# A block transpose moved behind the next row's sums, and mix weights loaded in parts

## The chip, the cores and the metric

The kernel runs on one core of a Trainium2 chip. The metric is the device time of one execution in microseconds; smaller is better. The engines are TensorE (PE in the profile, its weight loads PEld), VectorE (DVE), ScalarE (ACT), GpSimd (POOL) and SyncE (SP), which issues nearly all DMA transfers. Each engine works through its own list of instructions in order and waits at an instruction until what it needs is there.

## The reference, cut to what matters

The input x is 32 images of 56 x 56 tokens with 128 channels, all in f32. Two residual layers follow each other.

```
x = x + window_attention(group_norm(x))      # 7x7 windows shifted by 3, 4 heads of 32 channels
x = x + fourier_feedforward(group_norm(x))

window_attention(x):   qkv = x @ w_qkv.T per window of 49 tokens; softmax(q k^T * scale + bias + mask) v; @ w_proj.T + b
fourier_feedforward(x):
    along each of the two image axes: dct, keep 32 modes, mix channels per mode (w0 for one axis, w1 for the other), idct
    h = sum of both;  out = relu(h @ W1 + b1) @ W2 + b2          # 128 -> 512 -> 128
group_norm: 32 groups of 4 channels, statistics over the image
```

w0 and w1 have 128 x 128 x 32 numbers each, 2 MB. In the kernel their first use is in the Fourier layer of the first image.

## The kernel before, in words

Attention works on rows: one row is a strip of 7 lines of an image, 8 windows of 49 tokens, and an image has 8 rows. All images follow each other in one list of 256 rows. A loop over cycles starts one row per cycle and does older rows' later steps beside it. In cycle c:

- `attn_qk`, `attn_scores` and `attn_v` do row c on TensorE. ScalarE and VectorE move q and k out of PSUM (VectorE's half of k is L398), and VectorE adds the bias to the scores into `a` (L440).
- `attn_max` takes the maximum on VectorE (L450), and GpSimd subtracts it (L451). `attn_exp` is ScalarE's exponential (L457). `attn_divide` sums on VectorE (L462), takes the reciprocal (L464), and GpSimd multiplies twice (L467), first into `off_blocks`, then into `own_blocks`. Four SyncE transfers (L475, L476) then copy the 32 x 32 blocks that lie in the wrong partitions from `off_blocks` to `own_blocks`.
- `attn_transpose` is VectorE's block transpose of `own_blocks` into `eT` (L481). It waits for these copies. GpSimd may write `own_blocks` for the next row only when the transpose has read it.
- `attn_values` of row c - 3 multiplies `eT` with v on TensorE (L496), and ScalarE and VectorE move the result to `oT` (L528, L526). `attn_project` follows; VectorE adds it to the tokens in `xl` (L543). `attn_sums` of row c - 4 takes sums (L557) and sums of squares (L566) for the second layer's group norm.

In the first 11 cycles, `first_rows`, there is attention alone; in cycle c the exponential and the sums are those of row c - 1 and the transpose that of row c - 2. From cycle 11 on (`CONV_BEGIN`) the main loop also runs the Fourier layer of the image before: its statistics once per image (`fourier_stats`, a TensorE matmul that needs all L566 of the image), the transforms (L641), the mixing with w1 and w0 (L675), the way back (L714), and from the 9th cycle of an image on the feed-forward in two halves, `ff_in` and `ff_out` (L112), whose result VectorE adds to `res` (L783). Here the exponential and the sums in cycle c are those of row c itself, and the transpose that of row c - 1. The norm of the next image (`image_norm`) is spread over its steps; one of them is the small bias factor nb on VectorE (L362), whose matmul TensorE runs between attn_qk and ff_in.

The order on TensorE, ScalarE, VectorE and GpSimd is the order in which the code calls these functions; it is written by hand (`manual_schedule`). SyncE's order is made by the scheduler. Attention matmuls share four PSUM banks (pa) in rotation, the Fourier layer four others (pc), so a matmul waits until the bank that it gets has been emptied. The constants, w1sb and w0sb among them, are loaded in the order of the code on SyncE's queue (`const_load`, L134), behind image 1's load and ahead of the first row's block copies.

Of the kernel before, what the change touches and what calls it, by code (L numbers as in the profile page):

```python
# [10 lines left out]
F32 = mybir.dt.float32  # L11
# [4 lines left out]
P = 128  # L16
S = 56
C = 128
# [9 lines left out]
NM = 32  # L28
# [20 lines left out]
def swin_fourier_kernel(  # L49
# [20 lines left out]
    nc = tc.nc  # L70
    NB = x.shape[0]

    const = ctx.enter_context(tc.tile_pool(name="const", bufs=1))
# [46 lines left out]
    def load_image(b, parts=2):  # L120
        t = big.tile([TC, NCH, C], F32, tag="xl", name="xl", bufs=2)
        for k in range(parts):
            load_part(t, b, k)
        return t
# [7 lines left out]
    def const_load(shape, src, name):  # L132
        t = const.tile(shape, F32, tag=name, name=name)
        (nc.scalar if name in FIRST else nc.sync).dma_start(t, src)  # L134
        return t
# [21 lines left out]
    with nc.allow_non_contiguous_dma(reason="relative position bias, once"):  # L157
# [4 lines left out]
        for ix in range(WS):  # L162
            src = bass.AP(
                rpb_rev.tensor, rpb_rev.offset + WS - 1 - ix, [[span, NH * span], [1, WS]]
            )
# [44 lines left out]
    with nc.allow_non_contiguous_dma(reason="constant, once"):  # L210
        for blk in range(8):
# [4 lines left out]
            src = idct_h.rearrange("p (h r) -> p h r", r=4)[modes, :, 2 * li : 2 * li + 2]  # L216
# [2 lines left out]
    idcth = idcth.rearrange("p h r -> p (h r)")  # L219
    if NB > 1:  # L220
        xls[1] = load_image(1)
    w1sb = const_load([P, NM, C], w1, "w1sb")
    w0sb = const_load([P, NM, C], w0, "w0sb")
    wff1 = const_load([P, FF], W1, "wff1")
    b1sb = const_load([P, NF], b1.rearrange("(f p) -> p f", p=P), "b1sb")
    wff2 = const_load([P, NF, C], W2.rearrange("(f p) o -> p f o", p=P), "wff2")
# [41 lines left out]
    def image_groups(im, i):  # L268

        pt = [conv_bank() if i % 4 else attn_bank() for _ in range(2)]
        pts = [
            p[:, : n * S].rearrange("p (j r s) -> p j r s", r=n, s=WS) for p, n in zip(pt, (8, 6))
        ]
        for c in range(7):
            nc.tensor.transpose(
                pts[c // 4][:, :, 2 * (c % 4) : 2 * (c % 4) + 2],
                im.x[:, WS * i // 2 + c],
                ident_x[:, :, SS:].rearrange("p r (j s) -> p j r s", s=WS),  # L280
            )
        for k in range(2):

            im.xw[i + k] = big.tile([P, RT + JP - WT], F32, tag="xw", name="xw", bufs=10)
            nc.gpsimd.memset(im.xw[i + k][:, RT:], 0.0)
            xw = im.xw[i + k][:, :RT]
            dst = xw.rearrange("p (j r s) -> p j r s", r=WS, s=WS)
            if k:
                nc.scalar.copy(dst[:, :, 0], pts[0][:, :, WS])
                nc.scalar.copy(  # L290
                    dst[:, :, 1:].rearrange("p j r s -> p j (r s)"),
                    pts[1].rearrange("p j r s -> p j (r s)"),
                )
            else:
                nc.scalar.copy(
                    dst.rearrange("p j r s -> p j (r s)"),
                    pts[0][:, :, :WS].rearrange("p j r s -> p j (r s)"),
                )
            nc.vector.bn_stats(im.st[:, i + k], xw)
        if im.b > 1:  # L300
            image_bias(im, i)
# [157 lines left out]
    def attn_divide(r):  # L459
        a3 = a_sb[r % 2].rearrange("p t w j -> p (t w) j")  # L460
        sm = small.tile([P, 2 * NWR], F32, tag="sm", name="sm")
        nc.vector.tensor_reduce(sm, a3, axis=AX.X, op=ALU.add)  # L462
        rs = small.tile([P, 2 * NWR], F32, tag="rs", name="rs")
        nc.vector.reciprocal(rs, sm)  # L464
        for dst in (off_sb, own_sb):
            for k, (j0, n) in enumerate(((0, KB), (KB, WT - KB))):
                nc.gpsimd.tensor_tensor(  # L467
                    dst[:, k, :, :n],
                    a3[:, :, j0 : j0 + n],
                    rs.unsqueeze(2).to_broadcast([P, 2 * NWR, n]),  # L470
                    ALU.mult,
                )
        for p in range(0, P, JP):
            lo, hi = slice(p, p + KB), slice(p + KB, p + JP)
            nc.sync.dma_start(own_sb[lo, 1], off_sb[hi, 0])  # L475
            nc.sync.dma_start(own_sb[hi, 0], off_sb[lo, 1])  # L476

    def attn_transpose(im, i):

        eT = work.tile([P, NH * NP, JP], F32, tag="eT", name="eT")  # L480
        nc.vector.transpose(eT.rearrange("p t (k j) -> p k t j", k=2), own_sb)  # L481
        im.eT[i] = eT
# [334 lines left out]
    def row(r):  # L817
        return (images[r // NWR], r % NWR) if 0 <= r < NB * NWR else (None, 0)
# [12 lines left out]
    def load_back(cycle):  # L831
        for im, c in fourier(cycle):
            for width, g in back_groups(c):
                load_modes(im, width, g)
# [36 lines left out]
    def has_ff(cycle):  # L871
        return any(c in FF_AT for _, c in fourier(cycle))
# [37 lines left out]
        if im:  # L910
            attn_values(im, i, cycle - 3)

    def turn(cycle):
        im, i = row(cycle)
        if im:
            attn_transpose(im, i)

    def next_groups(cycle):
        b, i = divmod(cycle, NWR)
        if b + 1 < NB:  # L920
            for j in ({4: (0, 2), 5: (4, 6)} if b == 0 else {6: (0, 2, 4, 6)}).get(i, ()):
                image_groups(images[b + 1], j)
# [6 lines left out]
    def halves_last(cycle, norm):  # L929
        im, i = row(cycle)  # L930
        if im:
            attn_v(im, i, cycle)
        if has_ff(cycle):
            half_columns(cycle)
        half_columns(cycle, True)
        load_back(cycle + 1)
        next_begin(cycle)
        load_first(cycle)
        next(norm, None)
        if row(cycle)[0]:  # L940
            attn_exp(cycle)
            attn_divide(cycle)
        im, j = row(cycle - 3)
        if im:
            last_out(cycle)
            attn_project(im, j)
# [10 lines left out]
    def first_rows(cycle, norm):  # L957
        im, i = row(cycle)
        if im:
            attn_qk(im, i, True)  # L960
        if cycle:
            attn_exp(cycle - 1)
        im3, i3 = row(cycle - 3)
        if im3:
            attn_values(im3, i3, cycle - 3)
        turn(cycle - 2)
        if cycle:
            attn_divide(cycle - 1)
        if im:
            attn_scores(im, i, cycle)  # L970
            attn_max(cycle)
        if im3:
            attn_project(im3, i3)
        next(norm, None)
        last, j = row(cycle - 4)
        if last:
            for _ in attn_sums(last, j):
                pass
        if im:
            attn_v(im, i, cycle)  # L980

        if cycle < NWR // 2:
            image_bias(im, 2 * cycle)
        elif cycle >= NWR - 2 and cycle < NWR + 2:
            image_bias(images[1], 2 * (cycle - NWR + 2))
        if cycle in (4, 5):
            for half in range(2):
                bias_and_mask(nc.gpsimd, 1, cycle - 4, half)
        next_begin(cycle)
        next_groups(cycle)  # L990
        if cycle == CONV_BEGIN - 1:
            start_stats(im3)
            for _ in attn_sums(im3, i3):
                pass
            turn(cycle - 1)
            attn_exp(cycle)
            attn_divide(cycle)

    ET = mybir.EngineType
    with tc.manual_schedule(engines={ET.PE, ET.Activation, ET.DVE, ET.Pool}):  # L1000
        images[0] = image_begin(0)
        for i in range(0, NWR, 2):
            image_groups(images[0], i)
        norm = image_norm(images[0])
        for _ in range(3):
            next(norm)
        for cycle in range(NB * NWR + CONV_BEGIN + FF_AT[-1] - NWR + 1):
            if cycle < CONV_BEGIN:
                first_rows(cycle, norm)
            else:  # L1010
                halves_first(cycle, norm)
                if not row(cycle - 3)[0]:
                    half_columns(cycle)
                    half_columns(cycle, True)
                    load_first(cycle)
                    last_out(cycle)
                    quarters(cycle)
                    load_back(cycle + 1)
                    continue
                if not has_ff(cycle):  # L1020
                    half_columns(cycle)
                eighths(cycle)
                quarters(cycle)
                if not has_ff(cycle):
                    next(norm, None)
                if row(cycle)[0]:
                    attn_max(cycle)
                turn(cycle - 1)
                next_groups(cycle)
                halves_last(cycle, norm)  # L1030
            b, i = divmod(cycle, NWR)
            if i == (NWR - 2 if b else NWR - 3) and b + 1 < NB:
                norm = image_norm(images[b + 1])
                next(norm, None)
# [62 lines left out]
```

## Time and profile before

Three runs took 3543.2, 3557.74 and 3561.03 us; the median is 3557.74. The profiled execution has a span of 3546.4 us.

| engine | busy us | share of the span | instructions |
|---|---|---|---|
| PE | 3361.2 | 95% | 70144 |
| PEld | 2637.0 | 74% | 70144 |
| DVE | 2494.9 | 70% | 4722 |
| ACT | 1992.9 | 56% | 3788 |
| POOL | 1827.4 | 52% | 2204 |

Busy time is the time in which the engine had an instruction at work; what lies between is waiting, and the profile names the instruction on another engine, or the transfer, that ended each wait. In the slices of the span TensorE stands at 4, 6 and 8 tenths in the first three of forty and at 9 in all others. An image takes some 107 us in the steady part, a row 12 to 16 us.

The block transpose is one instruction per row: 256 of them with a mean of 1240 ns, 317.5 us in all. The sums before it in the new order are 963 ns in the mean, the reciprocal 253 ns.

### The profile page before, as it was taken

The numbers are of one execution on the slowest core, as the hardware profiler recorded it, in microseconds if no ns is written. First come the engines' busy times: TensorE is split into PE (matmuls) and PEld (weight loads), VectorE is DVE, ScalarE is ACT, GpSimd is POOL, SyncE is SP. The second block draws the span as 40 slices with busy tenths as digits, with TensorE's granted clock in tenths as the row PEclk, the third lists the DMA queues.
The fourth block names the chain that finished last, engine by engine and source line by source line (L and its number), as shares of the span: only waits on it lengthen the run. The fifth ranks groups of instructions, "written<-read, shape, count | busy, mean of one in ns | idle before, by whom it ended". The sixth has DMA issues, their size and how long they took to land.

```text
span 3546.4 us, 159605 instructions
## 1 busy us (share of the span) xinstructions
PE 3361.2 (95%) x70144; PEld 2637.0 (74%) x70144; DVE 2494.9 (70%) x4722; ACT 1992.9 (56%) x3788; POOL 1827.4 (52%) x2204
## 2 busy tenths in 40 slices
PE   4689999999999999999999999999999999999999
PEld 3567777777777777778777777777777777777776
DVE  4777777777777777776777776777776777777741
ACT  3455555555655555655555555555655555655553
POOL 4655554455555455554555554555554555554521
PEclk8799999999999999999999999999999999999999
DMA  4344555554555545555544555545555545555443
GB/s 116 86 112 118 138 129 142 132 125 127 136 132 143 134 120 132 137 131 138 136 126 128 134 132 135 138 120 135 132 133 137 136 122 131 137 135 135 119 132 98
DMA packets 736503, 457.35 MB, mean 129 GB/s; under 512 B 56351, under 2 KB 673984, under 8 KB 735552
## 3 DMA queue, kind: packets, MB, share of 16 engines
q1 hardware_dynamic: 735197, 446.82, 49.8%
q8 instruction: 551, 9.03, 1.1%
q14 instruction: 144, 1.18, 0.1%
q10 hardware_dynamic: 611, 0.32, 0.0%
HBM read 218.29 MB, written 161.48 MB: 107 GB/s over the span
## 4 chain that ended last, share of the span: by engine, by line
PE 45%; POOL 17%; DVE 13%; issue 10%; DMA 7%; ACT 4%; SPq 4%; POOLq 0%; DVEq 0%; ACTq 0%
PE pc L112 19%; PE pc L641 6%; PE pa L112 5%; POOL own_blocks L467 5%; POOL off_blocks L467 4%; DMA own_blocks<-off_blocks 4%; DVE sm L462 4%; PE pa L410 3%; POOL xl L308 3%; PE pc L675 3%; PE pa L432 3%; POOL a L451 2%; ACT a L457 2%; PE pa L496 2%; SPq L475 2%
## 5 line engine op out<-in xcount | busy, mean ns | idle before, releaser
L451 POOL TENSOR_TENSOR a<-a,mx 128x784 f32<-128x784 f32 x256 | 384.7, 1503 | 904.5 <-DVE mx L450 884.3
L467 POOL TENSOR_TENSOR off_blocks<-a,rs 128x512 f32<-128x512 f32 (+1 forms) x512 | 430.0, 861 | 644.7 <-DVE rs L464 441.6
L112 PE MATMUL pc<-wff,hid 128*64 128x128 f32 x12544 | 741.1, 273 | 4.5 <-issue 3.2
L112 PE MATMUL pc<-xf,wff 128*64 128x512 f32 (+2 forms) x3584 | 719.8, 539 | 1.0 <-DVE xf L725 1.0
L112 PEld LDWEIGHTS pc<-wff,hid 128*64 128x64 f32 x12544 | 703.5, 137 | 11.1 <-issue 5.1
L759 ACT ACTIVATE hid<-pc,b1sb 128x512 f32<-128x512 f32 (+2 forms) x896 | 515.0, 632 | 69.3 <-PE pc L112 67.5
L112 PEld LDWEIGHTS pc<-xf,wff 128*64 128x64 f32 x3584 | 286.0, 137 | 349.2 <-issue 223.2
L481 DVE STREAM_TRANSPOSE eT<-own_blocks 128x1024 f32<-128x1024 f32 x256 | 317.5, 1240 | 190.5 <-DMA own_blocks<-off_blocks 175.9
L467 POOL TENSOR_TENSOR own_blocks<-a,rs 128x512 f32<-128x512 f32 (+1 forms) x512 | 430.1, 862 | 0.0
L462 DVE TENSOR_REDUCE sm<-a 128x16 f32<-128x784 f32 x256 | 246.6, 963 | 254.2 <-ACT a L457 253.4
L112 PE MATMUL pa<-xw,wn 128*64 128x392 f32 (+1 forms) x2048 | 397.5, 503 | 18.6 <-ACT wn L365 9.2
L381 ACT ACTIVATE q<-pa,bqkv 128x392 f32<-128x392 f32 x256 | 149.8, 585 | 452.6 <-PE pa L112 448.4
L457 ACT ACTIVATE a<-a 128x784 f32<-128x784 f32 x256 | 219.0, 856 | 246.3 <-POOL a L451 238.3
L417 ACT COPY v<-pa 128x512 f32<-128x512 f32 x256 | 150.8, 589 | 342.6 <-PE pa L410 341.6
L526 DVE TENSOR_SCALAR oT<-pa,bqkv 128x147 f32<-128x147 f32 (+2 forms) x768 | 171.0, 279 | 219.5 <-PE pa L496 219.5
L747 POOL TENSOR_TENSOR res<-res,b2sb 128x512 f32<-128x512 f32 (+2 forms) x256 | 264.4, 1038 | 110.9 <-DMA res<-scr 102.7
L496 PEld LDWEIGHTS pa<-eT,v 49*32 49x32 f32 x16384 | 174.6, 106 | 167.5 <-issue 125.6
L410 PE MATMUL pa<-wn,xw 128*64 128x128 f32 x4096 | 287.5, 282 | 6.7 <-DVE oT L526 3.0
L308 POOL TENSOR_TENSOR xl<-xl,bproj 112x512 f32<-112x512 f32 (+1 forms) x256 | 287.4, 1146 | 0.0
L440 DVE TENSOR_TENSOR a<-pa,bm 128x392 f32<-128x392 f32 x512 | 264.6, 559 | 23.4 <-PE pa L432 4.2
L112 PE MATMUL pa<-wproj,oT 128*48 128x128 f32 (+1 forms) x3584 | 251.5, 276 | 10.7 <-ACT oT L528 7.3
L410 PEld LDWEIGHTS pa<-wn,xw 128*64 128x64 f32 x4096 | 224.2, 138 | 44.2 <-issue 8.8
(96 smaller groups left out, 5367.6 us busy)
## 6 DMA issues: line engine op xcount, KB each, us to landing
own_blocks<-off_blocks SPq DMA_DIRECT2D x1024, 64.0 KB
zscr<-z SPq DMA_DIRECT2D x512, 112.0 KB
htok<-scr SPq DMA_DIRECT2D x256, 196.0 KB
zT<-zscr SPq DMA_DIRECT2D x192, 256.0 KB
res<-scr SPq DMA_DIRECT2D x160, 256.0 KB
out_dram<-res SPq DMA_DIRECT2D x160, 256.0 KB
scr<-xl SPq DMA_DIRECT2D x128, 224.0 KB
xl<-in_x_dram SPq DMA_DIRECT2D x32, 784.0 KB
```

The source lines that it names most:

```text
L112: nc.tensor.matmul(dst[ps], lhsT=lhsT[:, ps], rhs=rhs, start=start, stop=stop)
L308: nc.gpsimd.tensor_tensor(piece, piece, bproj.unsqueeze(1).to_broadcast([TC, e - a, C]), ALU.add)
L410: nc.tensor.matmul(pv[hs, j * C : (j + 1) * C], lhsT=im.xw[i][:, w * WT : w * WT + JP], rhs=im.w[:, 2 * C : 3 * C], start=True, stop=True,)
L440: nc.vector.tensor_tensor(a[:, 2 * hp : 2 * hp + 2, :, 0:WT].rearrange("p u w j -> p w u j"), ps[hp][:, :RT].rearrange("p (w u j) -> p w u ...
L451: nc.gpsimd.tensor_tensor(a3, a3, mx.unsqueeze(2).to_broadcast([P, 2 * NWR, WT]), ALU.subtract)
L457: nc.scalar.activation(a2, a2, AF.Exp)
L462: nc.vector.tensor_reduce(sm, a3, axis=AX.X, op=ALU.add)
L467: nc.gpsimd.tensor_tensor(dst[:, k, :, :n], a3[:, :, j0 : j0 + n], rs.unsqueeze(2).to_broadcast([P, 2 * NWR, n]), ALU.mult,)
L481: nc.vector.transpose(eT.rearrange("p t (k j) -> p k t j", k=2), own_sb)
L496: nc.tensor.matmul(po4[u][h * HD : (h + 1) * HD, pr], lhsT=v[ks, pr, h * HD : (h + 1) * HD], rhs=eT[ks, h * NP + pr, :WT], start=True, sto ...
L747: nc.gpsimd.tensor_tensor(res[:m, c0:c1], res[:m, c0:c1], b2sb[:m].unsqueeze(1).to_broadcast([m, c1 - c0, C]), ALU.add,)
L759: nc.scalar.activation(hf[:, :n], ph[:, :n], AF.Relu, bias=b1sb[:, f : f + 1])
```

## The change

Two things are changed. First, the transpose of row r - 1 is now called inside `attn_divide` of row r, behind the sums and the reciprocal, in place of its own call ahead of them (`turn`, which goes away). It is meant to let the sums, and with them GpSimd's products, start without waiting for the copies of the row before, and to do the transpose while GpSimd fills `off_blocks`. The last row, which no sums follow, gets a call of its own. Second, w1 and w0 are no longer loaded whole among the constants, but in eight parts of 8 modes each (0.5 MB), one called in each of the cycles 2 to 9, so that the first row's block copies don't stand behind 4 MB.

```diff
-    w1sb = const_load([P, NM, C], w1, "w1sb")
-    w0sb = const_load([P, NM, C], w0, "w0sb")
+    w1sb = const.tile([P, NM, C], F32, tag="w1sb", name="w1sb")
+    w0sb = const.tile([P, NM, C], F32, tag="w0sb", name="w0sb")
+
+    def mix_weights(k):
+        dst, src = ((w1sb, w1), (w0sb, w0))[k // 4]
+        m = slice(k % 4 * NM // 4, (k % 4 + 1) * NM // 4)
+        nc.sync.dma_start(dst[:, m], src[:, m])
...
@@ attn_divide @@
         nc.vector.reciprocal(rs, sm)
+        im, i = row(r - 1)
+        if im:
+            attn_transpose(im, i)
         for dst in (off_sb, own_sb):
...
-    def turn(cycle):
-        im, i = row(cycle)
-        if im:
-            attn_transpose(im, i)
...
@@ halves_last @@
             attn_exp(cycle)
             attn_divide(cycle)
+        elif row(cycle - 1)[0]:
+            attn_transpose(*row(cycle - 1))
...
@@ first_rows @@
-        turn(cycle - 2)
         if cycle:
             attn_divide(cycle - 1)
...
+        if 1 < cycle < 10:
+            mix_weights(cycle - 2)
         if cycle == CONV_BEGIN - 1:
             start_stats(im3)
             for _ in attn_sums(im3, i3):
                 pass
-            turn(cycle - 1)
             attn_exp(cycle)
             attn_divide(cycle)
...
@@ main loop @@
                 if row(cycle)[0]:
                     attn_max(cycle)
-                turn(cycle - 1)
                 next_groups(cycle)
                 halves_last(cycle, norm)
```

## The prediction

> **What bounds the kernel now.** I read the page first, then the windows by stage, then the waits of TensorE, then the timeline row by row. The windows split the span in four: stalled start, first rows, first image's Fourier rows, steady part. Columns: length, busy time of each engine (instructions), granted clock, DMA share, GB/s.
>
> ```profile
> 37.00:61.00 24.00, 3.11 (x51) 1.65 (x51) 1.60 (x2) 3.07 (x5) 3.77 (x4) 0.66 0.90 277
> 61.00:152.00 91.00, 62.88 (x1320) 44.47 (x1318) 66.08 (x131) 37.30 (x72) 66.03 (x87) 0.79 0.22 56
> 152.00:245.00 93.00, 68.52 (x1444) 52.71 (x1444) 67.03 (x131) 46.71 (x93) 47.91 (x60) 0.87 0.45 112
> 245.00:3400.00 3155.00, 3067.45 (x64856) 2420.82 (x64858) 2308.62 (x4335) 1829.67 (x3479) 1673.99 (x2001) 1.00 0.52 132
> ```
>
> From 245 us on TensorE is idle 87.5 us in 3155, under 3%. There every wait of TensorE goes straight into the end time, and nothing on VectorE or GpSimd can win more than that 87.5. Before 245 us no engine is full; a chain of waits sets the pace. The waits (waiter, releaser, total us, times, longest) say which idle is at stake:
>
> ```profile
> DVE sm L462 <- ACT a L457: 253.4, 191, 4.3
> DVE eT L481 <- DMA own_blocks<-off_blocks: 175.9, 110, 23.8
> PE pa L112 <- DVE part L566: 28.4, 30, 1.4
> PE pa L112 <- DVE nb L362: 22.8, 29, 1.7
> PE pa L496 <- DVE eT L481: 19.9, 1, 19.9
> ```
>
> The transpose L481 waits much for its copies, but TensorE waits for the transpose only once, 19.9 us at the start. Its waits for part L566 and nb L362 come once per image in the steady part. The third view is VectorE's timeline around the second layer's statistics of a middle image, with TensorE's line that waits for it:
>
> ```profile
> 1517.36 0.96 DVE L450 TENSOR_REDUCE mx<-a 128x16 f32<-128x784 f32 x1
> 1518.24 1.24 DVE L481 STREAM_TRANSPOSE eT<-own_blocks 128x1024 f32<-128x1024 f32 x1
> 1520.83 0.97 DVE L462 TENSOR_REDUCE sm<-a 128x16 f32<-128x784 f32 x1 [1.35 <-ACT a L457]
> 1521.83 0.25 DVE L464 RECIPROCAL rs<-sm 128x16 f32<-128x16 f32 x1
> 1522.00 0.36 DVE L783 TENSOR_TENSOR res<-pc,res 128x256 f32<-128x256 f32 x1
> ...
> 1524.58 0.68 DVE L566 TENSOR_REDUCE part<-sq 112x32 f32<-112x512 f32 x1
> ...
> 1525.32 0.43 PE L112 MATMUL pa<-part,gmean 112*64 112x64 f32 x4 [1.03 <-DVE part L566]
> ```
>
> Between max and sums VectorE has to wait for GpSimd's subtraction (1.50) and ScalarE's exponential (0.86): some 2.5 us, in which the transpose of 1.24 lies free of charge. After the sums VectorE runs without a gap into the wait of TensorE.
>
> [...] the sums of row 1 had their input at 39.5 us and ran at 60.57, behind the transpose of row 0, which waited 23.83 for a copy. [...] the copies of row 0 landed at 59.3 us behind 4 MB of mix weights issued at 41.7 and 42.2. [...] eight matmuls L112 pa<-xw,wn take 2.88 us at 139.84 (clock 0.50) and 1.49 at 1519.26. [...] so I count TensorE's waits and not its 95%.
>
> **The change part by part.** No instruction is added but six DMA issues; the orders of TensorE, ScalarE and GpSimd stay the same. SyncE's order shifts in places, mostly own_blocks copies going ahead of a store of xl.
>
> *Weights in parts.* Ahead of row 0's own_blocks copies 4.19 MB leave the queue. What stays is image 1's load (1.61 MB), wff1, wff2 (0.52) and b2 (0.06): 2.19 MB at the 277 GB/s of the first window is 7.9 us from 37.2, so 45.1. Then four issues of 0.6 and a landing of 2.0: 49.5, and the transpose ends near 50.7 instead of 60.6. Gain 10 us (8 to 13). The parts are 0.52 MB each, 1.9 us at 277 GB/s. SyncE's order has three of them behind row 0's copies, three behind row 1's and two behind row 2's; those rows lie 7 us or more apart, so 5.7 us of loading fits between them (cost 0 to 2).
>
> *Transpose behind the sums, first rows.* Before, a row is this loop (chain of waits at 65 to 75 us): own_blocks done, SyncE 1.6, copy 2.0, transpose 1.25, sums and reciprocal 1.12, off_blocks 1.67, own_blocks 1.64, with latencies 9.6. Afterwards sums no longer wait for the copy, and the transpose lies beside off_blocks (1.25 beside 1.67). What waits behind the transpose is the score evictions L440, and through their banks the next qk matmuls. The new loop is max, subtract 1.50, exponential 0.86, sums 0.97, reciprocal 0.25, transpose 1.17, two evictions 1.0, max 0.97: 6.7, with latencies 7.0. GpSimd's loop through off_blocks and own_blocks is the same 7. The sums of row 1 are also done while row 0's copy is still out, so own_blocks of row 1 ends at about 53 (before 65.2) and of row 2 at 60 (74.9). From there to row 10, before: 76.9 us for eight rows. Afterwards: rows 3, 7 and 9, with a cold TensorE (9 us of its work per row at half clock), about 8; rows 4 and 5, with bn_stats of image 1, 8.4 of VectorE work; row 6, with its norm chain, 9.9 as before; rows 8 and 10, 7.5. Sum 66. Row 10 then ends at 126, 26 us earlier than 151.7. Were all rows but the three with norm work at 7.2 it would be 29, with a faster start 33; were the cold clock to hold in half the rows, 18.
>
> *Rows 11 to 18.* Where the copy was late (145.9, 207.7, 229.3) the sums gain 0.6 to 2.2; in rows 14, 17 and 19 the k eviction or the statistics get 1.17 later, and TensorE waits for both. Near 0.
>
> *Steady part.* Here the transpose leaves a hole and goes into a full stretch. In the hole 1.35 us of waiting becomes 2.5 and nobody gains: the sums still wait for the exponential. The stretch grows by 1.17 (the interval to the next instruction). Queued there: res L783, xl L543, part, k L398, part L566. I followed that 1.17 through every row of the timeline until an idle of VectorE took it up or TensorE was reached. In plain rows VectorE waits 0.7 to 1.7 before k, and k has slack of 0.8 to 2.6 before the scores: 5 us in all of them. At the statistics nothing takes it up: TensorE's wait grows from about 1.0 to 2.2, 30 images by 1.17, 35 us; up to 5 of it can fall on waits of L714 for its issue that follow. In the row of the next image's norm the short nb L362 no longer sits behind the transpose, and TensorE's wait for it, 22.8 us in all, goes; but the same row's k is then late: rs, transpose, res, xl, part, k end 1.17 later, and the slack before the scores is only 0.18 to 0.9. Net loss 0.74 a row, 29 rows, 21.5 us, of which up to 8 can fall on other waits. Total 5 + 35 + 21.5 less half of those 13: 55. As the two largest terms overlap waits that I can't see, I take 50 (35 to 62).
>
> GpSimd's own_blocks product, the one writer that the moved transpose could hold up, starts 1.7 us after the reciprocal, the transpose ends 1.25 after it: cost 0. The transpose now runs beside off_blocks instead of the subtraction; in the trace it takes 1.23 to 1.25 beside a busy and an idle GpSimd alike. eT is used two rows later, so its lateness costs nothing.
>
> Sum: 50 - 26 = +24 us on 3557.7, 3582.
>
> **The rivals.** *TensorE loses nothing in the steady part* (the delayed evictions are taken up by buffers that I read too strictly): only the start remains, 3558 - 26 = 3532. For it: VectorE is 73% busy there, and k has slack in most rows. Against it: the wait for part L566 exists already in 30 images, so whatever is put ahead of it counts in full. *They cancel*: the start gives 33 (warm rows) and the steady part takes 33 (statistics alone, norm rows neutral because nb comes early): 3558, within 0.5%. For it: nb's gain is as large as what I charge against it. *A new bound*: in the shortest rows, 12.05 us, VectorE's own loop becomes 9.9 of work and 2.5 of hole, 12.4; if that adds 0.35 in three rows of each image, 30 us more: 3611. Against it: the other rows of an image last 13 to 16 us and let VectorE catch up.
>
> **How the numbers follow.** Forecast 0.47, within 0.5% (3540 to 3575) by cancelling 0.24, only the start 0.17, the new bound 0.12. Slower is forecast plus new bound, 0.59. The costs' own ends give 35 - 33 = +2 to 62 - 18 = +44; the range is 3538 to 3606, which leaves out most of the faster case and the end of the slowest.
>
> **What would show it.** Right: own_blocks of row 0 lands near 49.5 us, the first rows last 7 to 8.5 us, TensorE is at the 245 us stage about 26 us earlier; the wait PE pa <- DVE part rises from 28 to about 63 us; the wait for nb vanishes and a wait of the scores or L112 for k or res stands in its place; the sums' wait for the exponential rises. Wrong: PE idle from the first feed-forward on stays at 3%, or the first rows stay at 9 us because TensorE is cold.

## The result and the profile after

The changed kernel takes 3603.87 us (median of 4 runs, 3600.03 to 3607.68), the kernel before beside it 3553.02 (4 runs, 3543.2 to 3561.03): ratio 1.0144, with a 95% interval of 1.0113 to 1.0176. It is slower by about 51 us. The forecast was 3582, with a range of 3538 to 3606.

The profiled executions span 3604.2 and 3546.4 us, so 57.8 us lie between the two traces. They are laid against each other at one landmark, TensorE's statistics matmul (`pa<-part,gmean`), which comes once per image. The first comes at 125.36 us (before 144.42), the second at 226.51 (before 245.08): here the change is 18.6 us ahead. From there to the end it needs 3377.7 us against 3301.3, 76.4 more.

The windows by stage of the changed kernel (length, busy time of PE, PEld, DVE, ACT and POOL, clock, DMA share, GB/s):

```profile
37.00:51.00 14.00, 1.83 (x14) 0.46 (x10) 2.21 (x3) 3.07 (x5) 4.26 (x5) 0.71 0.92 195
51.00:130.00 79.00, 56.93 (x1194) 41.73 (x1196) 66.67 (x130) 36.83 (x72) 64.42 (x85) 0.85 0.40 114
130.00:226.50 96.50, 71.26 (x1576) 56.53 (x1572) 66.90 (x131) 46.62 (x94) 49.44 (x61) 0.89 0.42 106
245.00:3400.00 3155.00, 3046.49 (x63345) 2391.15 (x63338) 2201.91 (x4255) 1785.42 (x3411) 1640.74 (x1966) 0.99 0.51 129
```

The stalled start ends 9.4 us earlier (the first transpose starts at 50.01 us, before at 59.40), and the first rows are denser. In the last line TensorE is idle 108.5 of 3155 us. Before it was 87.5, so idle has grown by only 21 us, far less than the loss. But in the same 3155 us TensorE does 63345 matmuls instead of 64856: it is busy and slower, and the clock column (1 is full speed) has gone from 1.00 to 0.99. The waits of the changed kernel show the idle part (waiter, releaser, total us, times, longest):

```profile
PE pa L112 <- DVE part L575: 41.6, 31, 1.4
PE pc L112 <- DVE res L792: 29.2, 48, 1.6
PE pa L416 <- ACT oT L537: 21.2, 30, 1.0
PE pa L505 <- DVE eT L490: 11.6, 1, 11.6
...
DVE sm L468 <- ACT a L463: 693.1, 252, 5.9
DVE eT L490 <- DMA own_blocks<-off_blocks: 12.5, 5, 10.3
```

L575 is the L566 of before, L792 is L783, L490 the transpose L481, L468 the sums L462. The wait for part has grown from 28.4 us, the wait for nb (22.8) is gone, and the waits for res and, at L416, for oT are new. VectorE's wait for the exponential has gone from 253.4 to 693.1 us: the hole between maximum and sums is now empty. The same place as in the timeline of before, ahead of the statistics of a middle image:

```profile
1527.66 0.96 DVE L456 TENSOR_REDUCE mx<-a 128x16 f32<-128x784 f32 x1
1531.12 0.97 DVE L468 TENSOR_REDUCE sm<-a 128x16 f32<-128x784 f32 x1 [2.50 <-ACT a L463]
1532.12 0.25 DVE L470 RECIPROCAL rs<-sm 128x16 f32<-128x16 f32 x1
1532.30 1.25 DVE L490 STREAM_TRANSPOSE eT<-own_blocks 128x1024 f32<-128x1024 f32 x1
1533.47 0.39 DVE L792 TENSOR_TENSOR res<-pc,res 128x256 f32<-128x256 f32 x1
...
1536.08 0.68 DVE L575 TENSOR_REDUCE part<-sq 112x32 f32<-112x512 f32 x1
```

From the reciprocal to the start of the statistics matmul it was 3.49 us (1521.83 to 1525.32); now it is 4.69 (1532.12 to 1536.81). That is the transpose's interval of 1.17 to within 0.03. TensorE's timeline at the same place:

```profile
1533.91 1.08 PE L112 MATMUL pc<-xf,wff 128*64 128x512 f32 x4 [0.30 <-DVE res L792]
1535.12 0.34 PE L112 MATMUL pa<-tot,gmean 112*64 112x64 f32 x4
1536.81 0.43 PE L112 MATMUL pa<-part,gmean 112*64 112x64 f32 x4 [1.35 <-DVE part L575]
1537.17 0.81 PE L505 MATMUL pa<-eT,v 49*32 49x49 f32 x64
1537.91 1.58 PE L438 MATMUL pa<-k,q 64*64 64x98 f32 x32
1539.27 2.31 PE L723 MATMUL pc<-idctw,zT 64*64 64x112 f32 x48
1541.52 1.09 PE L416 MATMUL pa<-wn,xw 128*64 128x128 f32 x16
```

The wait is spread over res (0.30) and part (1.35). Then something follows that no list of waits shows: the 32 matmuls of the scores take 1.58 us and the 48 of the way back 2.31, where the kernel before took 0.90 and 1.33:

```profile
1526.42 0.90 PE L432 MATMUL pa<-k,q 64*64 64x98 f32 x32
1527.14 1.33 PE L714 MATMUL pc<-idctw,zT 64*64 64x112 f32 x48
```

Windows over this stretch of the changed kernel give the clock (third number from the right):

```profile
1536.81:1537.60 0.79, 0.79 (x50) 0.62 (x52) 0.27 (x2) 0.61 (x2) 0.23 (x1) 1.00 0.34 83
1537.60:1541.50 3.90, 3.90 (x112) 3.70 (x108) 2.71 (x10) 0.44 (x1) 0.55 (x1) 0.56 0.32 79
```

In windows of a quarter of a microsecond the clock stands at 0.50 from 1537.9 to 1541.3, for 3.4 us. In the kernel before scores and way back together take about 2.2 us behind each statistics from the third on, and the clock stays at 1.00 in all 29 images. In the changed one they take 3.3 us or more, at half clock, in 24 of 29.

A table by rows puts the loss in its place. Each number is the time from the first scores matmul of a row to that of the next, taken from the timeline and averaged over 28 images (rows 27 to 250):

| from row | holds | before | after | difference |
|---|---|---|---|---|
| 0 | | 14.25 | 14.12 | -0.13 |
| 1 | | 10.10 | 10.17 | +0.07 |
| 2 | statistics wait | 13.10 | 14.36 | +1.26 |
| 3 | the matmuls behind it | 16.65 | 17.31 | +0.66 |
| 4 | | 13.77 | 13.60 | -0.17 |
| 5, 6 | | 24.47 | 24.43 | -0.04 |
| 7 | next image's norm | 14.35 | 15.18 | +0.83 |
| sum | | 106.68 | 109.18 | +2.50 |

How far two traces of one code differ, e1 below shows, which from row 11 on runs the code of the kernel before: its rows 2 and 3 are the same to 0.02 us, but row 4 has 14.05, row 7 14.55 and the sum is 107.16. So the differences of rows 2 and 3 stand, that of row 7 is known to some 0.3 us, and those of rows 0, 1, 4, 5 and 6 say nothing.

Over 29 images 2.50 is 72.5 of the 76.4 us. So the theory to test: the statistics wait costs 36.5 us, the half clock behind it some 19, the norm row 24 (18 against e1's trace), and the start brings 18.6.

### The profile page after: what moved, and what is told of

The parts are those of the page before. It is cut to its first block, busy times and chain, and to the rows that moved or that the text cites. A ratio compares the mean times of both kernels' runs of the same rounds, so it can differ in the third digit from the quotient of the medians.

```text
span 3604.2 us, 159553 instructions
## 1 busy us (share of the span) xinstructions
PE 3407.1 (95%) x70144; PEld 2664.0 (74%) x70144; DVE 2432.4 (67%) x4722; ACT 1988.8 (55%) x3788; POOL 1826.9 (51%) x2204
## 4 chain that ended last, share of the span: by engine, by line
PE 58%; DVE 13%; issue 10%; POOL 9%; ACT 6%; DMA 2%; SPq 1%; DVEq 0%; POOLq 0%; ACTq 0%
PE pc L112 22%; PE pa L112 7%; PE pc L684 6%; PE pc L650 6%; PE pa L416 5%; PE pa L438 4%; DVE sm L468 3%; DVE eT L490 3%; PE pc L723 3%; PE pa L505 3%; POOL own_blocks L476 3%; ACT a L463 3%; POOL a L457 3%; ACT hid L768 2%; POOL res L756 1%
## 5 line engine op out<-in xcount | busy, mean ns | idle before, releaser
L112 PE MATMUL pc<-xf,wff 128*64 128x512 f32 (+2 forms) x3584 | 730.5, 541 | 30.4 <-DVE res L792 29.2
L468 DVE TENSOR_REDUCE sm<-a 128x16 f32<-128x784 f32 x256 | 248.3, 970 | 693.1 <-ACT a L463 693.1
L112 PEld LDWEIGHTS pc<-xf,wff 128*64 128x64 f32 x3584 | 273.2, 137 | 402.4 <-issue 218.8
L490 DVE STREAM_TRANSPOSE eT<-own_blocks 128x1024 f32<-128x1024 f32 x256 | 318.8, 1245 | 13.1 <-DMA own_blocks<-off_blocks 12.5
L416 PE MATMUL pa<-wn,xw 128*64 128x128 f32 x4096 | 288.1, 283 | 24.4 <-ACT oT L537 21.2
L416 PEld LDWEIGHTS pa<-wn,xw 128*64 128x64 f32 x4096 | 225.3, 139 | 63.3 <-ACT oT L537 27.1
L574 ACT ACTIVATE sq<-xl 112x384 f32<-112x384 f32 (+1 forms) x256 | 146.2, 571 | 220.5 <-DVE xl L552 215.2
```

The source lines that it names most:

```text
L112: nc.tensor.matmul(dst[ps], lhsT=lhsT[:, ps], rhs=rhs, start=start, stop=stop)
L416: nc.tensor.matmul(pv[hs, j * C : (j + 1) * C], lhsT=im.xw[i][:, w * WT : w * WT + JP], rhs=im.w[:, 2 * C : 3 * C], start=True, stop=True,)
```

## The experiments

Times are beside runs of the kernel before on the same chip. Against it the changed kernel stands at 1.0144.

### The two halves apart

`e1_weights_only` is the kernel before with the loads in eight parts. `e2_move_only` is the changed kernel with w1 and w0 loaded whole, among the constants:

```diff
-    w1sb = const.tile([P, NM, C], F32, tag="w1sb", name="w1sb")
...
+    w1sb = const_load([P, NM, C], w1, "w1sb")
+    w0sb = const_load([P, NM, C], w0, "w0sb")
...
-        if 1 < cycle < 10:
-            mix_weights(cycle - 2)
```

> The weights are loaded in eight parts, the transposes stay where they were in the kernel before. Theory (the two halves of the change work apart; the loads only shift the first copies): row 0's transpose ends near 51 us instead of 59.4, nothing else changes, 8 to 12 us faster than the kernel before. Rival (the parts get in the way of later rows' copies and take back what they give): within 3 us of the kernel before. Rival (the parts are what costs in the changed kernel): slower.

> The transposes are behind the sums in all rows, the weights are loaded whole as in the kernel before. Theory (the loss of the changed kernel, 76 us from the second statistics on, is the move's alone): slower than the changed kernel by the 8 to 12 us of the weights, so 58 to 65 us slower than the kernel before. Rival (weights in parts disturb the steady part): less than 40 us slower than the kernel before.

Measured: e1 3547.66 us, ratio 0.9982 (0.9973 to 0.9991); e2 3608.23 us, ratio 1.0167 (1.0148 to 1.0187). In e1's trace the first transpose starts at 50.15 us instead of 59.40 and the second statistics matmul comes at 235.58, 9.5 us early. The time is 6.4 us shorter (3.2 to 9.6): the expectation of 8 to 12 holds in the start, and for the whole the interval is too wide to tell. In e2 the landmark comes at 234.66, 10.4 us early, and the kernel is 59 us slower. So the loss belongs to the move, and at the start the two halves add up: 9.5 and 10.4, against 18.6 together.

### The move in the first rows only

```diff
@@ attn_divide @@
-        if im:
+        if im and not (r >= CONV_BEGIN):
             attn_transpose(im, i)
@@ main loop @@
                     attn_max(cycle)
+                    if cycle >= CONV_BEGIN:
+                        attn_transpose(*row(cycle - 1))
                 next_groups(cycle)
```

> The changed kernel, but from row 11 on the transposes lie behind the maximum again. Theory (start gains, steady part loses by the move): the 18.6 us of the start stay and the 76 us vanish, 15 to 22 us faster than the kernel before, images 106.4 us apart as before. Rival (the stretch was only one cause, the shifted issue order or the loads another): images stay above 107 us, not faster than the kernel before.

Measured: 3527.16 us, ratio 0.9945 (0.9926 to 0.9964), 20 us faster than the kernel before by the ratio (the medians are 25 apart). The second statistics matmul comes at 222.41, 22.7 us early, 4 us more than in the changed kernel. The intervals of rows 2 and 3 are back at 13.12 and 16.68 us. Row 7 is at 14.69 and the sum at 107.23, as in e1's trace (14.55 and 107.16) and half a microsecond above the trace of before; the profiled run, 3541.03 us, was also the slowest of the six. With the transpose back in its place the steady part loses nothing that the time would show, so its loss is the move's.

### TensorE kept busy in the wait

```diff
         for k, t in enumerate(rows):
             t = t.rearrange("p k g -> p (k g)")
+            for _ in range(0 if k else 3):
+                halved(pg[:, : C // 2], gmean, t)
             halved(pg[:, : C // 2], gmean, t, start=(k == 0), stop=(k == 1))
```

> The changed kernel, but the first of the two matmul groups of the statistics (tot, 0.34 us) is done four times over, the first three for nothing, so that TensorE works through about 1.0 of the 1.35 us for which it waits for part. Theory (about half of the 76 us is that TensorE falls to half clock after this wait, some 1.6 us in each of 24 images, 38 us in all): scores and inverse transform behind the statistics take 0.90 and 1.33 us again instead of 1.58 and 2.31, and the kernel is 25 to 38 us faster than the changed one, though it does more. Rival (the wait alone costs, the slow matmuls are covered by what follows): within 5 us of the changed kernel. Rival (the wait itself grows by the added work): slower than it by up to 10 us.

Measured: 3586.87 us, ratio 1.011 (1.009 to 1.013), with twelve matmuls more per image faster than the changed kernel: 17 us by the medians, 12 by the ratios, whose intervals just overlap. The traces say it more sharply. The timeline of TensorE in e4 behind a statistics wait:

```profile
1418.38 1.08 PE L112 MATMUL pc<-xf,wff 128*64 128x512 f32 x4 [0.30 <-DVE res L794]
1419.59 0.69 PE L112 MATMUL pa<-tot,gmean 112*64 112x64 f32 x16
1421.28 0.43 PE L112 MATMUL pa<-part,gmean 112*64 112x64 f32 x4 [1.00 <-DVE part L575]
1421.64 0.81 PE L505 MATMUL pa<-eT,v 49*32 49x49 f32 x64
1422.38 0.90 PE L438 MATMUL pa<-k,q 64*64 64x98 f32 x32
1423.11 1.33 PE L725 MATMUL pc<-idctw,zT 64*64 64x112 f32 x48
```

The sixteen matmuls take 0.69 us, not four times 0.34, so they fill only 0.35 of the wait; 1.00 remains. From tot to part it is 1.69 us in both kernels: the wait of VectorE's making is untouched. Yet scores and way back run at full clock again in 26 of 29 images, and the interval of row 3 falls from 17.31 to 16.48. That shows the half clock and prices it: 0.83 us an image in that row, 24 us, of which some 20 remain in the sum over all rows (109.18 to 108.50) and 12 to 17 in the time. Not all of the slowness is lost: from the statistics matmul to the v matmuls it is 4.41 us in the changed kernel and 3.28 in e4 (means of 29 images), but from there to the forward transform 1.03 and 1.22. At full clock TensorE arrives before VectorE has evicted xf and waits again (0.14 us in most images of e4), at half clock that wait is covered. My expectation of 25 to 38 us had left such waits out.

### One transpose in eight put back

e5, e6 and e10 are the changed kernel with the old place for one row of each image. The edit is that of e3 with `r % NWR == 2` (6, 7) added to the condition.

> The changed kernel, but in one row of eight, the one whose sums VectorE does right ahead of the second layer's statistics (row 2 of an image), the transpose lies behind the maximum again. Theory (the loss sits where the longer stretch ends in a wait of TensorE: 1.26 us an image in the interval that holds the statistics and 0.66 in the next one at half clock): both intervals return to 13.1 and 16.7 us, images shrink from 109.2 to 107.3 us, the kernel is 45 to 56 us faster than the changed one, near the kernel before. Rival (each of the eight transposes costs its share, the statistics only show it): an eighth of the loss, 9 us faster than the changed one.

> The changed kernel, but in the row whose sums come right ahead of the next image's norm chain (row 6) the transpose lies behind the maximum again. Theory (there xl is 1.17 us later, so ScalarE's square waits for it, and behind the square in ScalarE's queue stand the hid and oT for which TensorE waits 0.70 us in 30 images): this wait goes and the interval from row 7 to row 8 shrinks from 15.18 to about 14.5 us, 15 to 21 us faster than the changed kernel. Rival (k behind the transpose makes the scores late, as the prediction has it, or the wait only moves on to the wait for res 12 us later): within 5 us of the changed kernel.

> The changed kernel, but in row 7 of each image, the row of the norm chain itself, the transpose lies behind the maximum again. Theory (after e6: the interval from row 7 to row 8 is set by VectorE's chain from the scores over maximum, exponential, sums and transpose to the eviction res, for which ff_in waits; whatever ends earlier ahead of it only waits longer): the wait for res in that row goes, a part of the wait for nb comes back, and the interval shrinks from 15.18 to between 14.35 and 14.7 us, 14 to 24 us faster than the changed kernel, although the wait for oT (0.70) stays. Rival (oT and res cost only together, neither alone): within 5 us of the changed kernel.

| put back | time us | ratio | row 2 | row 3 | row 7 |
|---|---|---|---|---|---|
| none (changed kernel) | 3603.87 | 1.0144 (1.0113 to 1.0176) | 14.36 | 17.31 | 15.18 |
| row 2 (e5) | 3556.94 | 1.0007 (0.9995 to 1.002) | 13.13 | 16.67 | 15.15 |
| row 6 (e6) | 3607.29 | 1.0148 (1.0124 to 1.0171) | 14.40 | 17.06 | 15.27 |
| row 7 (e10) | 3568.99 | 1.0051 (1.0037 to 1.0065) | 14.36 | 17.06 | 14.26 |

e5: one transpose of the eight is worth 47 us. Both intervals return to those of before and no image falls to half clock behind the statistics. e6 went to the rival. Its waits:

```profile
PE pc L112 <- DVE res L792: 54.0, 47, 2.4
PE pa L112 <- DVE part L575: 41.6, 31, 1.4
```

The wait for oT is gone, and the wait for res has taken all of it, 54.0 us instead of 29.2. I had read the first of two waits in one row as a loss of its own. Which of the two sets the row, e10 shows:

```profile
PE pa L112 <- DVE part L575: 41.6, 31, 1.4
...
PE pa L416 <- ACT oT L537: 23.4, 31, 1.1
...
PE pc L112 <- DVE res L792: 5.8, 20, 0.3
...
PE pa L112 <- DVE nb L368: 1.2, 3, 0.7
```

Here the wait for oT stands as it was, the wait for res falls to 5.8 us, and the interval of row 7 shrinks by 0.92. So the row is set by VectorE's chain from the scores to res, with the transpose in it. What TensorE does in between only decides how long it waits at its end. nb hardly comes back, presumably because TensorE reaches it later, behind the wait for oT. The 35 us gained are more than expected (14 to 24). The interval gives 27 of them over 29 images; fewer images at half clock (17 of 29, row 3 at 17.06) lie on top.

### The transpose ahead of the sums, behind nb

```diff
@@ attn_divide @@
+        im, i = row(r - 1)
+        if im and r >= CONV_BEGIN:
+            attn_transpose(im, i)
         sm = small.tile([P, 2 * NWR], F32, tag="sm", name="sm")
...
-        if im:
+        if im and r < CONV_BEGIN:
             attn_transpose(im, i)
```

> Weights in parts and the first rows of the changed kernel; from row 11 on the transpose stands directly ahead of the sums, behind whatever else is queued after the maximum, nb of the next image's norm above all. It differs from e3_move_first_rows only in the order of nb and one transpose of an image. Theory (the hole hides the transpose, and nb is 1.4 us earlier): TensorE's wait for nb (22.8 us in 29 images) goes, without a wait for res in its place, 18 to 24 us faster than e3_move_first_rows, 40 to 46 us faster than the kernel before. Rival (what TensorE gains at nb it waits at the next eviction): within 5 us of e3_move_first_rows.

Measured: 3523.41 us, ratio 0.9908 (0.9888 to 0.9927), 33 us faster than the kernel before. This is the fastest version tried. The waits of e3 and of e7:

```profile
PE pa L112 <- DVE part L575: 27.3, 31, 1.4
PE pa L112 <- DVE nb L368: 25.9, 29, 2.1
```

```profile
PE pa L112 <- DVE part L577: 28.2, 31, 1.4
PE pc L112 <- DVE res L794: 13.3, 28, 1.2
```

The wait for nb is gone, half of it has come back as a wait for res. The interval of row 7 falls from 14.69 to 14.06, 18 us in 29 images; by the ratios e7 is 13 us ahead of e3, where 18 to 24 were expected. This lies between theory and rival, for the reason found with e10: with nb out of the way the row runs into the next wait of the same chain.

### VectorE's own work in the first rows

e9 changes what the sums of the first rows read, e11 does them twice:

```diff
 # e9: attn_sums, called by first_rows with short=True
+        if short:
+            n1 = n0 + 1
...
 # e11: attn_sums, called by first_rows with times=2; both reductions
+        for _ in range(times):
             nc.vector.tensor_reduce(
```

> The changed kernel, but the partial sums of the first image's rows 0 to 6 are taken over one of the three or four slices of a row (so these sums are not the reference's), which takes some 0.6 to 0.8 us of VectorE's work from each of seven first rows. Theory (VectorE's own work, with xl, the partial sums and oT that the prediction left out of its loop, sets the pace of the first rows): the first image's statistics matmul comes 4 to 5.5 us earlier than at 125.4 us. Rival (a cold TensorE or the copies set it): under 1.5 us earlier.

> The changed kernel, but both partial sums of the first image's rows 0 to 6 are reduced twice, 0.9 to 1.2 us more of VectorE's work in each of seven first rows, 7 to 8 us in all, after e9_short_partial_sums had left its question half open (3.1 us earlier). Theory (VectorE's own work sets the pace of the first rows): the first image's statistics matmul comes 5 to 8 us later than at 125.4 us, and the kernel is that much slower. Rival (copies and a cold TensorE set most rows): under 3 us later.

Measured: in e9 the part reductions ahead of the first statistics matmul take 5.26 us instead of 9.8, 4.5 less, and the matmul comes at 122.25 instead of 125.36, 3.1 us earlier. In e11 they take 18.8, 9.0 more, and it comes at 130.37, 5.0 later. The time of e11 shows nothing of this: 3603.08 us, ratio 1.0142 (1.0124 to 1.016), the interval being as wide as the effect. (e9 has a single run, 3592.67 us.) In six other kernels with the same first rows the landmark lies between 123.8 and 127.4 us, so e9 alone would prove little. Both directions together, 8.1 us between e9 and e11 for 13.5 us of work, say that somewhat more than half of VectorE's work there counts: the theory holds in part, and so does its rival. Windows of e11 (DVE busy is the third):

```profile
75.00:85.00 10.00, 7.40 (x178) 5.50 (x178) 9.68 (x19) 7.60 (x17) 7.93 (x19) 1.00 0.35 94
85.00:95.00 10.00, 6.89 (x136) 5.18 (x136) 9.59 (x26) 4.12 (x9) 6.57 (x13) 0.83 0.29 77
```

VectorE is full there. In the changed kernel's own rows it is nearly so from 66 to 102 us, and less so from 102 to 111 us, where TensorE's clock is 0.68:

```profile
85.00:94.00 9.00, 5.37 (x144) 3.81 (x139) 8.62 (x24) 4.74 (x8) 7.46 (x9) 1.00 0.23 56
...
102.00:111.00 9.00, 7.13 (x137) 4.71 (x138) 5.89 (x14) 4.00 (x7) 6.47 (x7) 0.68 0.23 56
```

## Why the prediction was right, and where its numbers were off

The direction, the mechanism and the place of the loss were right: the transpose leaves a hole and enters a full stretch, and TensorE pays at the statistics and in the norm row. The time is 22 us above the forecast and only 2 us inside the range. That it lies inside is partly luck: the loss in the steady part, 76.4 us by the two traces and about 70 by the times (51 and the 18.6 of the start), is beyond the 62 that the prediction gave as its upper end. By its own steps:

*Weights in parts.* Predicted: transpose of row 0 ends near 50.7, gain 10. It ended at 51.2; e1 gains 9.5 us at the second statistics. Right.

*Transpose behind the sums, first rows.* Row 2's own_blocks were forecast for 60; the trace has them end at 60.08. Right. From row 2 to row 10 it takes 69.5 us (reciprocals at 56.69 and 126.22), against 76.9 before and 66 forecast, 8.7 a row. The term that was mis-sized is "the new loop", 6.7 us: it counts maximum, sums, reciprocal, transpose and evictions but leaves out VectorE's other work in the same row, xl, the partial sums and oT. That is 3.5 us of the 26. e9 and e11 show that somewhat more than half of this work is on the path; what makes up the rest stays open, and one trace is loose here: in the six other kernels with the same first rows the stretch takes 67.5 to 71.4 us.

*Rows 11 to 18, "near 0".* They cost some 3 us: from the reciprocal of row 10 to the second statistics it is 97.0 us in the kernel before, 97.8 in e3 and 100.3 in the changed kernel. So the start brought 18.6. e5, which of these rows puts back row 18 alone, needs 97.9: the loss sits in the row ahead of the second statistics, as it does in the later images.

*Steady part, statistics, 35 us.* The interval of row 2 grew by 1.26 an image, 36.5 us, and the reciprocal-to-matmul distance by 1.20. Right. The profile's wait for part itself rose only to 41.6 and not to 63, since the rest shows as the wait for res ahead of it and as later tot: the sign that I had given was too narrow, the sum was not.

*What was missing* is the half clock behind that wait, the largest single cause of the 22 us: 19 us in the interval of row 3 (24 by e4's trace, 12 to 17 by its time). This is a term that the prediction put at nothing. It reckoned with a lower clock in the first rows alone, and which of them would have it was an estimate. It counted a longer wait as a longer wait, and never asked what clock TensorE would have after it. In the image shown TensorE waited 1.35 us, and from 1.1 us after that wait its clock stood at 0.50 for 3.4 us.

*Norm rows, 21.5 us.* Measured +0.83 an image, 24 us (+0.63 and 18 against e1's trace): the size is right, and so is nb vanishing. The path was wrong: not "k late before the scores", which hardly appears among the waits (0.2 us from 250 to 3400 us), but the chain from the scores through the transpose to res, as e10 shows and e6 shows from the other side.

*Less half of 13 that falls on other waits, and overlap.* I took 50 instead of 55. Statistics and norm row came in full, 60 us together. The plain rows, charged 5 us, gave 8 back in these two traces (-0.27 over the five other intervals), which is no more than traces of one code differ by. Together with the half clock this is the 72.5.

The rivals: *TensorE loses nothing* and *they cancel* fall with e5 and e10. The *new bound* fails too: the shortest rows, 1, 5 and 6, grew by 0.03 us together (10.10 and 24.47 before) and not by 0.35 each.

Open: why two of the images keep the full clock behind a wait that brings 24 others down (the last section has three more), and what makes row 7 differ by 0.2 to 0.3 us between traces of the same order.

## What to carry to other kernels

On an engine that is not the bottleneck, ask of each instruction not how long it takes but whether it stands in a hole or in a stretch at whose end the bottleneck engine waits: of eight equal moves per image one was worth 47 us, one 35, another nothing. When TensorE's idle time doesn't account for a loss, compare the duration of the same group of matmuls and the clock column: a stall can cost again in what runs after it, here 12 to 17 us by e4's time. And use an order where it helps only: the move in the first rows, with the transpose in the hole and behind nb everywhere else, beats both kernels.

## What the runs showed of the hardware

- TensorE's clock fell to 0.50 behind short waits. With a wait of 1.35 us for part, in most images some 2 us after one of 0.30 for res, it fell in 24 of 29 images; with 1.00 in place of the 1.35 (e4) in 3 of 29; with at most 1.03 and none for res (before) in none of 29. In the image shown the slow stretch begins 1.1 us after the stall has ended and lasts 3.4 us, so the work that was slowed is not only what waited: the scores took 1.58 us instead of 0.90, the way back 2.31 instead of 1.33.
- Three of the five images that kept their clock have the wait in another place. In the changed kernel's trace every change of the clock lies on a grid of 3.413 us (to within 6 ns), and each slow stretch behind the statistics of these 29 images is one step of it. In 26 of 29 images the whole wait of 1.35 us lies in one step, in which TensorE is busy for 48 to 60%; the next step has a clock of 0.50 in 24 of them. In three images (883.13, 1866.34, 2849.14 us) an edge of the grid cuts the wait, both steps are busy for 63 to 84%, and the clock stays at 1.00. In the kernel before no such step is busy for less than 70%, and the clock stays at 1.00 in all 29.
- The busy share alone doesn't settle it: the images at 336.25 and 1755.99 us, neither with the wait for res, kept the clock at 56 and 57%, and in e4 some images kept it at 58 to 67% (the one at 1421.28 us at 58%) and three lost it at 67% (the one at 1529.17 us among them).
- Twelve more matmuls of 112 x 64 inside a wait took 0.35 us by the profile and nothing from the chain; they made the kernel 12 to 17 us faster.
